# First score unit of each attention set in front of the last projected block of the stage before, in a decoder layer on one core

## The chip, the core and the metric

The kernel runs on one core of one Trainium2 chip. Five engines work side by side, each through its own queue in order: PE (TensorE: matrix products, with its weight loads shown apart as PEld), DVE (VectorE), ACT (ScalarE), POOL (GpSimd) and SP (SyncE, which here issues transfers). Products land in PSUM, from where DVE or ACT move them to SBUF. The metric is the device time of one execution in microseconds (us).

## What is computed

One decoder layer over four sequences (b = 0 to 3) of 512 rows and 512 columns in float32, with 16 heads of 32:

```
x = x + self_attention(layernorm(x))          # causal, projections q, k, v, o with biases
x = x + cross_attention(layernorm(x), ctx, ctx)   # causal mask of -10000; keys and values are ctx itself
x = x + ffn(layernorm(x))
ffn(x) = relu(x @ W_up.T) @ W_down.T + sum(softmax(top2(x @ W_gate.T))) * (x @ W_expert)
```

Softmax subtracts the largest score of each row, so every attention makes its scores twice: once by query to find the maxima, and once by key to take exponentials.

## The kernel before

The rows and the columns are cut into four blocks of 128 each. A projected block is four products of 128x128 by 128x512 (`project` or `project_t`); in the trace each such float32 product is two records.

**Order.** The order on PE, DVE, ACT and POOL is the order in which the program issues its instructions (`tc.manual_schedule`). For each sequence b the self attention and then the cross attention run through two functions. `with_maxima` makes the maxima of one attention in ten units and puts products of another stage between the units, so that the engines that work on the scores have time. `attend` then makes the exponentials and the values in ten further units.

**A unit.** In both functions a unit takes one or two pieces (g, i): g is a group of four heads, i a block of 128 rows or columns. Its scores go to two tiles of PSUM, each a `pair` of banks; four pairs exist in all (`ps`, bufs=4) and go round in the order in which the program gives them up. In `maxima` ACT copies each of the two tiles to SBUF (L304, tag `pt`, six buffers), POOL masks the diagonal (L312), and DVE reduces (L324), as `jobs` that are issued while the next unit's products are. After the last piece of a group, `split` writes its maxima as three bfloat16 parts (L345 to L350), `rows` turns them by PE (L361) and a copy puts them in SBUF (L367). In `scores` PE makes the scores (L405) and subtracts the maxima (L416), ACT takes the exponential of each tile (L439), and POOL clears the masked half (L447).

**What stands between.** `steps` is the list of blocks that `with_maxima` spreads over its units by `due`: for the first self attention two query and key blocks and all values (`query_key`, `value`); for the self attentions of b = 1 and 2 the `ffn` of the sequence before (`share`, `up`, `gate`, `down`); for that of b = 3 expert blocks and two `up` blocks; for the cross attentions the query and key blocks of the next sequence, in b = 1 with expert blocks of b = 0 behind them, and in b = 3 the rest of the `ffn` of b = 2. Two neighbouring blocks of `value`, `up`, `down` and `expert`, and query and key of one block of columns, share one pair and are moved to SBUF together: values and `down` by DVE's additions (L685, L843), experts by DVE (`weigh`, L867, which also issues the output transfer on SP), `up` by ACT (L790), queries and keys by ACT (L645, L648), and the last two `down` rows of b = 2 by ACT (`aside`, L861), whose addition POOL does later out of `put_off`.

**The entry of `attend`.** It starts when all blocks are done. Units 0, 1 and 2 are scored in a row; then the values of unit 0 (L482) follow, then unit 3, the maxima of the group or groups that `late` names (L361 again), the values of unit 1, unit 4 and so on. The pair of a group's values is held until that group is finished. DVE adds up exponentials over the blocks of a group (`add_up`, L552), and PE sums them over rows (L558).

Of the kernel before, what the change touches and what calls it, by code (L numbers as in the profile page):

```python
# [26 lines left out]
def decoder_layer(  # L27
# [21 lines left out]
    nc = tc.nc  # L49
# [579 lines left out]
            nc.gpsimd.tensor_tensor(e.x[:, t, :], e.x[:, t, :], bo_sb, ALU.add)  # L629

    def query_key(e):
        b, made = e.b, {}
        e.q_t = act.tile([P, NC, S], F32, tag="q_t", name=f"qT_{b}")
        e.k_t = act.tile([P, NC, S], F32, tag="k_t", name=f"kT_{b}")

        def query(f):
            made[f] = pair(f"pm_qk{b}_{f}")
            yield from project_t(made[f][:, 0, :], wq_sb, e.xn_t, f)

        def key(f):  # L640
            yield from project_t(made[f][:, 1, :], wk_sb, e.xn_t, f)
            out(f)

        def out(f):
            nc.scalar.activation(  # L645
                e.k_t[:, f, :], made[f][:, 1, :], AF.Identity, bias=bk_sb[:, f : f + 1]
            )
            nc.scalar.activation(  # L648
                e.q_t[:, f, :],
                made[f][:, 0, :],  # L650
                AF.Identity,
                bias=bqs_sb[:, f : f + 1],
                scale=SCALE,
            )

        def half(n):

            if n == 0:
                made[0] = pair(f"pm_qk{b}_0")
            rows = slice(n * S // 2, (n + 1) * S // 2)  # L660
            for c in range(NC):
                nc.tensor.matmul(
                    made[0][:, 0, rows],
                    lhsT=wq_sb[:, c, :P],
                    rhs=e.xn_t[:, c, rows],
                    start=(n == 0 and c == 0),
                    stop=(n == 1 and c == NC - 1),
                    skip_group_check=True,
                )

        steps = [(lambda f=f, w=w: w(f)) for f in range(NC) for w in (query, key)]
        if b == 0:
            steps[:1] = [lambda: half(0), lambda: half(1)]
        return steps

    def value(e):
        b, made = e.b, {}
        e.v = act.tile([P, NT, D], F32, tag="v", name=f"v_{b}")

        def one(t):  # L680
            if t % 2 == 0:
                made[0] = pair(f"pm_v{b}_{t}")
            yield from project(made[0][:, t % 2, :], e.xn_t, wv_sb, t)
            if t % 2 == 1:
                nc.vector.tensor_tensor(  # L685
                    e.v[:, t - 1 : t + 1, :],
                    made[0],
                    bv_sb.unsqueeze(1).to_broadcast([P, 2, D]),
                    ALU.add,
                )  # L690

        return [(lambda t=t: one(t)) for t in range(NT)]
# [85 lines left out]
    def ffn(e):  # L778
        b, f_t, made = e.b, e.f_t, {}

        def up(f):
            if f == 0:
                made["h"] = act.tile(
                    [P, NC, S], F32, tag="o_t" if b != B - 2 else "f_t", name=f"hT_{b}"
                )
            if f % 2 == 0:
                made["u"] = pair(f"pm_u{b}_{f}")
            yield from project_t(made["u"][:, f % 2, :], wup_sb, f_t, f)
            if f % 2 == 1:
                nc.scalar.activation(made["h"][:, f - 1 : f + 1, :], made["u"], AF.Relu)  # L790
# [41 lines left out]
            nc.vector.tensor_reduce(made["rw"], ew, axis=AX.X, op=ALU.add)  # L832

        def down(t):
            if t % 2 == 0:
                made["d"] = pair(f"pm_d{b}_{t}")
            yield from project(made["d"][:, t % 2, :], made["h"], wdown_sb, t)
            if t == NT - 1 and b == B - 2:
                for n in range(2):
                    aside(f"d{b}_{n}", t - 1 + n, made["d"][:, n, :])  # L840
            elif t % 2 == 1:
                both = e.x[:, t - 1 : t + 1, :]
                nc.vector.tensor_tensor(both, made["d"], both, ALU.add)  # L843

        def expert(t):
            if b == B - 1 and t == NT - 1:
                yield from expert_parts(t)
                return
            last = b == B - 1 and t == NT - 2
            if t % 2 == 0:  # L850
                made["e"] = pair(f"pm_e{b}_{t}")
            yield from project(made["e"][:, t % 2, :], f_t, wexp_sb, t)
            for n in (0,) if last else (0, 1) if t % 2 == 1 else ():
                u = t - t % 2 + n
                weigh(u, made["e"][:, n, :], slice(0, D), nc.sync)

        def aside(name, t, ps):


            some = work.tile([P, D], F32, tag="xn", name=f"some_{name}", bufs=4)  # L860
            nc.scalar.copy(some, ps)  # L861
            xt = e.x[:, t, :]
            put_off.append(lambda: nc.gpsimd.tensor_tensor(xt, xt, some, ALU.add))
# [41 lines left out]
    def with_maxima(steps, a, first=0, norms=()):  # L905


        norms = list(norms)
        run(steps[:first])
        fill = matmuls(steps[first:])  # L910
        total = sum(1 if step.__name__ in ("share", "gate") else NC for step in steps[first:])

        units = []
        for g in range(0, NC, 2):
            units += [[(g, 1), (g + 1, 1)]]
            units += [u for k in (g, g + 1) for u in ([(k, 2), (k, 0)], [(k, NT - 1)])]

        lead = 2 if first else 0
        for _ in range(lead):
            next(fill)  # L920
        done, due, jobs, late = lead, float(lead), [], {3: NC - 1}
        todo = []
        for n, pieces in enumerate(units):
            new = a.maxima(pieces)
            if todo:
                todo.pop()(nc.gpsimd)
            if norms and n % 2 == 0:
                new.append(norms.pop(0))
            due += (total - lead) / len(units)

            count = round(due) - done
            for k in range(count):
                next(fill, None)
                done += 1
                if k == min(1, count - 1) and n in (5, 7):
                    jobs = a.rows((n - 5) // 2) + jobs
                if k == min(1, count - 1) and a.cross and n in (6, 8):
                    todo.append(a.masked(*a.masked_sums((n - 6) // 2)))
                if n == len(units) - 1 and k == count - (2 if count > 4 else 1):
                    if total >= 2 * len(units):  # L940
                        if a.cross:
                            a.rows(2)[0](nc.scalar.copy)
                    else:
                        late = {3: 2, 5: NC - 1}
                run(jobs[:1])
                jobs = jobs[1:]
            run(jobs)
            jobs = new
        for _ in fill:
            pass  # L950
        run(jobs)
        return late

    def attend(a, late):


        units = []
        for g in range(0, NC, 2):
            units += [[(g, 0)], [(g, 3), (g, 1)], [(g, 2), (g + 1, 2)]]
            units += [[(g + 1, 0)], [(g + 1, 3), (g + 1, 1)]]  # L960
        waiting, held, todo = [], [], []

        def values():
            made = waiting.pop(0)
# [8 lines left out]
                if waiting[0][0][1] == 2 and waiting[0][1][0] == a.joined:  # L973
                    a.join(waiting[0][1], waiting[1][0])

        for n, pieces in enumerate(units):
            waiting.append(a.scores(pieces))
            if n in late:
                two = a.cross and late[n] == NC - 1
                together = not a.cross and len(late) == 1  # L980
                both = pair(f"mt_{a.name}_both") if two or together else None
                copies = a.rows(2, both, 1) if together else []
                copies += a.rows(late[n], both)

                more = [a.masked_sums(2, both)] if two else []
                for copy in copies:
                    copy(nc.scalar.copy)
                todo.extend(a.masked(*each) for each in more)
            if a.cross and n == 7:
                todo.append(a.masked(*a.masked_sums(3)))  # L990
            if n in (4 if a.joined is None else 6, 6, 9) and todo:
                todo.pop(0)()
            if n in (3, 4) and put_off:
                put_off.pop(0)()
            if len(waiting) > 2:
                values()
        while waiting:
            values()
# [1 line left out]
    with tc.manual_schedule(engines=BY_HAND):  # L1000
# [11 lines left out]
        for b in range(B):  # L1012
# [2 lines left out]
            norms, turns = [], []  # L1015
            if more:
                after, norms, turns = norm_in(b + 1)
            late = with_maxima(between_self, sa, skip, norms)
            if b == B - 1:
                e.x = load_x(b)  # L1020
            attend(sa, late)
            if b > 0:
                add_bias(e)
            made = out_projection(e, sa, context(e) + turns)
# [4 lines left out]
            norm_cross(e, made, 2)  # L1029
            ca = Attention(e.cq_t, e.ck_t, e.cv, True, f"c{b}")  # L1030
            ca.e, ca.out = e, e.beh_t
            late = with_maxima(steps[3:], ca)
            if b + 2 < B:
                after.x = load_x(b + 1)
            attend(ca, late)
            if more:
                cvs[b + 1] = load_cv(b + 1)
            filler = value(after) if more else ahead
# [73 lines left out]
```

## Time and profile before

Three runs took 803.87, 804.10 and 805.67 us, median 804.1. The profiled execution is one further execution; of it the span is known, 803.7 us from its first to its last instruction, and no time of its own beside that. TensorE's granted clock was 0.998 over it.

| stretch, us | what it is | length | PE busy | DVE busy | ACT busy | POOL busy |
|---|---|---|---|---|---|---|
| 27.5 to 66.7 | maxima, self, b = 0 | 39.2 | 39.20 | 28.94 | 21.63 | 14.43 |
| 66.7 to 77.3 | entry of its `attend` | 10.6 | 10.39 | 10.45 | 8.55 | 5.55 |
| 126.3 to 157.3 | maxima, cross, b = 0 | 31.0 | 31.00 | 24.85 | 24.03 | 13.08 |
| 157.3 to 168.1 | entry of its `attend` | 10.8 | 10.44 | 10.06 | 10.18 | 8.97 |
| 309.5 to 354.4 | maxima, cross, b = 1 | 44.9 | 44.90 | 26.36 | 25.24 | 14.76 |
| 676.3 to 706.3 | maxima, cross, b = 3 | 30.0 | 30.00 | 25.74 | 21.83 | 13.60 |

A line of the timeline gives the start, the duration, the engine, the line of the kernel, the operation, what it writes and reads, its shape, and the number of instructions merged; in square brackets stands the idle time of the engine before it and what ended it. The ends of PE's instructions are modelled, so the distance from start to start says more than the duration. In the names, `sm` are scores for maxima, `sc` scores for exponentials, `pv` values, `mt` turned maxima, `mb` maxima summed for the masked part of the cross attention, `pm` projected blocks; `_s` is self, `_c` cross.

### The profile page before, as it was taken

How to read it: one execution, taken by the hardware profiler on the slowest of the kernel's cores; microseconds unless marked ns; L12 is line 12 of the kernel's file. 1: busy time of each engine (PE TensorE's matmuls, PEld its weight loads, DVE VectorE, ACT ScalarE, POOL GpSimd, SP SyncE). 2: the span in 40 equal slices, each digit the busy share in tenths (PEclk: the TensorE clock that was granted, in tenths of full speed). 3: DMA queues.
4: the chain of work that ended last, by engine and by line, in shares of the span. 5: the costliest groups of instructions: out<-in, count | busy, mean ns of one | idle time of the engine just before them, and what ended most of it. 6: DMA issues, size and time to landing. Idle time of an engine off the chain costs nothing.

```text
span 803.7 us, 13927 instructions
## 1 busy us (share of the span) xinstructions
PE 794.0 (99%) x5588; PEld 378.9 (47%) x5592; DVE 565.9 (70%) x963; ACT 395.2 (49%) x448; POOL 339.6 (42%) x523
## 2 busy tenths in 40 slices
PE   8999999999999999999999999999999999999998
PEld 6444454444444454444544455444444444444544
DVE  2378855889679854678867786588959766988512
ACT  2457516871456615567055742687156833674110
POOL 3434612564234732257332482256423652475100
PEclk9999999999999999999999999999999999999999
DMA  9710000001010000021100000000102000000101
GB/s 301 275 28 1 2 1 1 2 27 54 1 27 2 2 0 1 2 78 55 53 14 14 1 2 0 1 1 2 53 28 80 2 1 1 1 2 1 53 1 52
DMA packets 15282, 24.51 MB, mean 30 GB/s; under 512 B 2033, under 2 KB 5361, under 8 KB 15217
## 3 DMA queue, kind: packets, MB, share of 16 engines
q1 hardware_dynamic: 14496, 22.96, 8.6%
q8 instruction: 44, 0.72, 0.4%
q10 hardware_dynamic: 720, 0.66, 0.2%
q14 instruction: 22, 0.17, 0.1%
HBM read 19.42 MB, written 4.19 MB: 29 GB/s over the span
## 4 chain that ended last, share of the span: by engine, by line
PE 95%; ACT 2%; issue 1%; DMA 1%; DVE 0%; ACTq 0%
PE pm_qk L241 14%; PE pm_d L229 7%; PE pm_u L241 7%; PE pm_v L229 7%; PE pm_o L725 7%; PE pm_e L229 7%; PE pv_c L482 6%; PE pv_s L482 6%; PE sm_c L293 6%; PE sm_s L293 6%; PE sc_s L405 5%; PE sc_c L405 5%; PE sc_s L416 1%; PE sc_c L416 1%; PE tp_a L255 1%
## 5 line engine op out<-in xcount | busy, mean ns | idle before, releaser
L324 DVE TENSOR_REDUCE nm_s<-s_s 128x2 f32<-128x1024 f32 (+3 forms) x128 | 96.9, 810 | 34.7 <-POOL s_s L312 34.7
L324 DVE TENSOR_REDUCE nm_c<-s_c 128x2 f32<-128x1024 f32 (+3 forms) x128 | 95.8, 810 | 31.0 <-POOL s_c L312 31.0
L304 ACT COPY s_s<-sm_s 128x1024 f32<-128x1024 f32 x80 | 77.1, 1015 | 70.7 <-PE sm_s L293 36.7
L304 ACT COPY s_c<-sm_c 128x1024 f32<-128x1024 f32 x80 | 77.1, 1016 | 35.9 <-PE sm_c L293 16.2
L312 POOL TENSOR_SCALAR_AFFINE_SELECT s_c<-s_c 128x512 f32<-128x512 f32 (+1 forms) x80 | 43.9, 550 | 100.4 <-ACT s_c L304 100.4
L312 POOL TENSOR_SCALAR_AFFINE_SELECT s_s<-s_s 128x512 f32<-128x512 f32 (+1 forms) x80 | 43.8, 551 | 94.4 <-ACT s_s L304 94.4
L552 DVE TENSOR_TENSOR sum_s<-sum_s,pt_s 128x256 f32<-128x256 f32 (+2 forms) x72 | 59.9, 897 | 15.4 <-PE pv_s L482 15.4
L439 ACT ACTIVATE pt_c<-sc_c 128x1024 f32<-128x1024 f32 x64 | 61.7, 1031 | 18.1 <-PE sc_c L416 10.1
L447 POOL TENSOR_SCALAR_AFFINE_SELECT pt_c<-pt_c 128x512 f32<-128x512 f32 (+1 forms) x64 | 52.9, 833 | 20.7 <-ACT pt_c L439 20.2
L229 PE MATMUL pm_d<-wdown_sb,hT 128*128 128x512 f32 x128 | 61.5, 611 | 0.0
L241 PE MATMUL pm_qk<-xnT,wk_sb 128*128 128x512 f32 x128 | 61.0, 606 | 0.0
L241 PE MATMUL pm_u<-fT,wup_sb 128*128 128x512 f32 x128 | 59.3, 605 | 0.0
L439 ACT ACTIVATE pt_s<-sc_s 128x1024 f32<-128x1024 f32 x56 | 53.9, 1030 | 10.5 <-POOL pt_s L447 5.5
L229 PE MATMUL pm_v<-wv_sb,xnT 128*128 128x512 f32 x128 | 58.8, 600 | 0.0
L725 PE MATMUL pm_o<-wo_sb,oT_s 128*128 128x512 f32 x128 | 57.8, 596 | 0.0
L405 PE MATMUL sc_c<-cqT,ckT 32*128 32x384 f32 (+3 forms) x512 | 56.4, 464 | 0.9 <-ACT sum_c L439 0.9
L241 PE MATMUL pm_qk<-xnT,wq_sb 128*128 128x512 f32 x120 | 56.7, 605 | 0.0
L229 PE MATMUL pm_e<-wexp_sb,fT 128*128 128x512 f32 x120 | 56.3, 604 | 0.0
L447 POOL TENSOR_SCALAR_AFFINE_SELECT pt_s<-pt_s 128x512 f32<-128x512 f32 (+1 forms) x56 | 48.0, 865 | 16.9 <-ACT pt_s L439 16.2
L405 PE MATMUL sc_s<-qT,kT 32*128 32x128 f32 (+3 forms) x512 | 54.1, 464 | 0.9 <-ACT sum_s L439 0.9
L293 PE MATMUL sm_c<-ckT,cqT 32*128 32x512 f32 (+3 forms) x512 | 47.5, 460 | 0.0
L293 PE MATMUL sm_s<-kT,qT 32*128 32x512 f32 (+3 forms) x512 | 47.0, 461 | 0.0
(171 smaller groups left out, 1268.1 us busy)
## 6 DMA issues: line engine op xcount, KB each, us to landing
cv<-in_ctx_dram SPq DMA_DIRECT2D x16, 256.0 KB, 4.4
out_dram<-x SPq DMA_DIRECT2D x15, 256.0 KB, 2.0
xin<-in_x_dram SPq DMA_DIRECT2D x12, 256.0 KB, 2.8
x<-in_x_dram SPq DMA_DIRECT2D x12, 256.0 KB, 4.2
wq_sb<-in_wq_dram SPq DMA_DIRECT2D x2, 512.0 KB, 6.7
wk_sb<-in_wk_dram SPq DMA_DIRECT2D x2, 512.0 KB, 7.7
wv_sb<-in_wv_dram SPq DMA_DIRECT2D x1, 1024.0 KB, 7.8
wo_sb<-in_wo_dram SPq DMA_DIRECT2D x1, 1024.0 KB, 9.5
```

Of the source, the lines that this page charges most:

```text
L229: nc.tensor.matmul(pm, lhsT=lhs_t[:, c, t * P : (t + 1) * P], rhs=w[:, c, :], start=(c == 0), stop=(c == NC - 1),)
L241: nc.tensor.matmul(pm, lhsT=w[:, c, f * P : (f + 1) * P], rhs=rhs_t[:, c, :], start=(c == 0), stop=(c == NC - 1),)
L293: nc.tensor.matmul(scs[r // 2][:, r % 2, c : c + (i + 1) * P], lhsT=self.q_t[h, g, i * P : (i + 1) * P], rhs=self.k_t[h, g, : (i + 1) * P] ...
L304: nc.scalar.copy(s, scs[n])
L312: nc.gpsimd.affine_select(out=diagonal, in_=diagonal, compare_op=ALU.is_ge, fill=NEG, base=0, pattern=[[0, 2], [0, len(pieces)], [-1, P]], ...
L324: nc.vector.tensor_reduce(self.nm[g][:, i, 2 * n : 2 * n + 2], made[n][:, :, c : c + (i + 1) * P], axis=AX.X, op=ALU.max, negate=True,)
L405: nc.tensor.matmul(scs[r // 2][:, r % 2, c : c + S - j * P], lhsT=self.k_t[h, g, j * P : (j + 1) * P], rhs=self.q_t[h, g, j * P :], start= ...
L439: nc.scalar.activation(pt, scs[n], AF.Exp)
L447: nc.gpsimd.affine_select(out=diagonal, in_=diagonal, compare_op=ALU.is_ge, fill=0.0, base=0, pattern=[[0, 2], [0, len(pieces)], [1, P]], ...
L482: nc.tensor.matmul(pv[r * HD : (r + 1) * HD, u, j * P :], lhsT=ones if u else self.v[:, j, h * HD : (h + 1) * HD], rhs=pts[r // 2][:, r % ...
L552: nc.vector.tensor_tensor(to, to, pts[n][:, :, c : c + S - j * P], ALU.add)
L725: nc.tensor.matmul(pms[t // 2][:, t % 2, :], lhsT=a.out[:, c, t * P : (t + 1) * P], rhs=wo_sb[:, c, :], start=(c == 0), stop=(c == NC - 1),)
```

## The change

Five edits, all in the order of work and in the use of PSUM pairs:

- `with_maxima` takes the last block out of the list that it spreads over the units: four products fewer stand between the units. After the units and the blocks that are left it issues score unit 0 of the attention, then the four products of the last block, with the reductions of the last maxima unit between them, and in an early cross attention the turned maxima of group 2. It returns unit 0 as `begun`.
- `attend` starts with `begun`, scores unit 1, and issues the values of unit 0 right behind it; unit 2 has no values behind it, and from unit 3 on the order is as before.
- The first stage issues six products instead of two before its first maxima unit.
- The last two blocks of a stage no longer share a pair, nor one instruction that moves them: the values 2 and 3 of b = 0, the first two `up` of b = 2, the last two `down` of b = 0 to 2, the experts 2 and 3 of b = 0, and query and key 3 of b = 1 and 3.
- Where the last query and key are apart, the query is moved right after its products.

```diff
     def query_key(e):
-        b, made = e.b, {}
+        b, made, apart = e.b, {}, (NC - 1,) if e.b % 2 else ()
...
         def query(f):
             made[f] = pair(f"pm_qk{b}_{f}")
             yield from project_t(made[f][:, 0, :], wq_sb, e.xn_t, f)
+            if f in apart:
+                out_query(f)
 
         def key(f):
-            yield from project_t(made[f][:, 1, :], wk_sb, e.xn_t, f)
-            out(f)
-
-        def out(f):
+            if f in apart:
+                pm = pair(f"pm_k{b}_{f}")[:, 0, :]
+            else:
+                pm = made[f][:, 1, :]
+            yield from project_t(pm, wk_sb, e.xn_t, f)
             nc.scalar.activation(
-                e.k_t[:, f, :], made[f][:, 1, :], AF.Identity, bias=bk_sb[:, f : f + 1]
-            )
+                e.k_t[:, f, :], pm, AF.Identity, bias=bk_sb[:, f : f + 1]
+            )
+            if f not in apart:
+                out_query(f)
...
+            if b == 0 and t >= NT - 2:
+                pm = pair(f"pm_v{b}_{t}")[:, 0, :]
+                yield from project(pm, e.xn_t, wv_sb, t)
+                nc.vector.tensor_tensor(e.v[:, t, :], pm, bv_sb, ALU.add)
+                return
...
+            if b == B - 2 and f < 2:
+                pm = pair(f"pm_u{b}_{f}")[:, 0, :]
+                yield from project_t(pm, wup_sb, f_t, f)
+                nc.scalar.activation(made["h"][:, f, :], pm, AF.Relu)
+                return
...
         def down(t):
+            if t >= NT - 2 and b < B - 1:
+                pm = pair(f"pm_d{b}_{t}")[:, 0, :]
+                yield from project(pm, made["h"], wdown_sb, t)
+                if b == B - 2:
+                    aside(f"d{b}_{t}", t, pm)
+                else:
+                    nc.vector.tensor_tensor(e.x[:, t, :], pm, e.x[:, t, :], ALU.add)
+                return
...
+            if b == 0 and t >= NT - 2:
+                pm = pair(f"pm_e{b}_{t}")[:, 0, :]
+                yield from project(pm, f_t, wexp_sb, t)
+                weigh(t, pm, slice(0, D), nc.sync)
                 return
...
     def with_maxima(steps, a, first=0, norms=()):
-        norms = list(norms)
-        run(steps[:first])
-        fill = matmuls(steps[first:])
-        total = sum(1 if step.__name__ in ("share", "gate") else NC for step in steps[first:])
...
-        lead = 2 if first else 0
+        norms = list(norms)
+        run(steps[:first])
+        fill, last = matmuls(steps[first:-1]), matmuls(steps[-1:])
+        total = sum(1 if step.__name__ in ("share", "gate") else NC for step in steps[first:-1])
+        early = total + NC >= 2 * len(units)
+
+        lead = 6 if first else 0
         for _ in range(lead):
             next(fill)
-        done, due, jobs, late = lead, float(lead), [], {3: NC - 1}
+        late = {3: NC - 1} if early else {3: 2, 5: NC - 1}
+        done, due, jobs = lead, float(lead), []
...
-                if n == len(units) - 1 and k == count - (2 if count > 4 else 1):
-                    if total >= 2 * len(units):
-                        if a.cross:
-                            a.rows(2)[0](nc.scalar.copy)
-                    else:
-                        late = {3: 2, 5: NC - 1}
...
         for _ in fill:
             pass
+        begun = [a.scores([(0, 0)])]
+        for k in range(NC):
+            next(last)
+            if k == 1 and a.cross and early:
+                a.rows(2)[0](nc.scalar.copy)
+            run(jobs[:1])
+            jobs = jobs[1:]
+        for _ in last:
+            pass
         run(jobs)
-        return late
+        return begun, late
...
-        waiting, held, todo = [], [], []
+        waiting, held, todo = list(begun), [], []
...
-        for n, pieces in enumerate(units):
+        for n, pieces in enumerate(units[1:], 1):
             waiting.append(a.scores(pieces))
...
-            if len(waiting) > 2:
+            if n == 1 or n > 2:
                 values()
```

## The prediction

> **What bounds the kernel now.** I read the page first: one engine is busy for the whole span.
>
> ```profile
> span 803.7 us, 13927 instructions
> PE 794.0 (99%) x5588; PEld 378.9 (47%) x5592; DVE 565.9 (70%) x963; ACT 395.2 (49%) x448; POOL 339.6 (42%) x523
> ```
>
> A busy PE is not a PE at its peak, and the view of waits gives PE almost none. So I read the start times in the timeline. The entry of the first self attention (PE, then ACT, then DVE):
>
> ```profile
> 66.70 1.14 PE L405 MATMUL sc_s<-qT,kT 32*128 32x512 f32 x8
> ...
> 69.16 0.70 PE L405 MATMUL sc_s<-qT,kT 32*128 32x256 f32 x4
> 70.07 0.92 PE L405 MATMUL sc_s<-qT,kT 32*128 32x256 f32 x10 [0.21 <-ACT sum_s L439]
> ...
> 71.35 1.07 PE L482 MATMUL pv_s<-sum_s,v 128*32 128x512 f32 x8
> 72.35 1.17 PE L405 MATMUL sc_s<-qT,kT 32*128 32x512 f32 x6
> ...
> 74.10 0.62 PE L361 MATMUL mt_s_both<-identb,parts 128*128 128x128 bf16 x8
> 74.65 1.07 PE L482 MATMUL pv_s<-pt_s,v 128*32 128x128 f32 x16
> 75.65 1.50 PE L405 MATMUL sc_s<-qT,kT 32*128 32x128 f32 x16
> ...
> 77.29 1.07 PE L482 MATMUL pv_s<-pt_s,v 128*32 128x256 f32 x16
> ```
>
> ```profile
> 68.08 1.94 ACT L439 ACTIVATE sum_s<-sc_s 128x1024 f32<-128x1024 f32 x2 [2.08 <-PE sc_s L416]
> 69.91 3.78 ACT L439 ACTIVATE pt_s<-sc_s 128x1024 f32<-128x1024 f32 x4
> 74.02 1.94 ACT L439 ACTIVATE sum_s<-sc_s 128x1024 f32<-128x1024 f32 x2 [0.33 <-PE sc_s L416]
> ```
>
> ```profile
> 66.81 1.23 DVE L685 TENSOR_TENSOR v<-pm_v,bv_sb 128x1024 f32<-128x1024 f32 x1
> ...
> 69.79 2.33 DVE L324 TENSOR_REDUCE nm_s<-s_s 128x2 f32<-128x1024 f32 x2
> 72.16 0.45 DVE L346 CAST parts<-nm_s 128x16 bf16<-128x16 f32 x1
> ```
>
> Score units 0 to 2 take 66.70 to 71.35, 4.65 us. An undisturbed unit takes 1.29 after values (79.28 to 80.56), 1.07 of it work; three in a row need 3.43. Units 3 and 4 take 1.75 and 1.64. So each entry, from unit 0 to the third values, takes 10.59 us, some 2.0 of it held by PSUM: four pairs of banks go round, and a unit needs two that ACT has emptied. All eight entries show 10.59, but c0 and c2 10.72, where ACT is late with keys and queries. In front of them, a unit of maxima with k products costs 1.07+0.20+0.86k: 2.98 for two (126.36 to 129.34), 3.84 for three. Where only one product stands between two units (the last cross attention), PSUM holds PE there too:
>
> ```profile
> 701.18 1.13 PE L229 MATMUL pm_d<-wdown_sb,hT 128*128 128x512 f32 x2
> 702.14 0.38 PE L374 MATMUL mb_c<-mrow_c,same 128*128 128x512 bf16 x1
> 702.45 1.98 PE L293 MATMUL sm_c<-ckT,cqT 32*128 32x512 f32 x8
> 704.36 1.98 PE L229 MATMUL pm_d<-wdown_sb,hT 128*128 128x512 f32 x4
> ```
>
> The last unit takes 1.91 instead of 1.07: its second half waits for ACT's copy of the unit before (to 703.26).
>
> I call the attentions s0, c0, s1 ... c3. The program hands PSUM pairs out in the order in which it gives them up. I follow that order by hand below, with the durations above. Median 804.1 is 0.4 above the profiled span; the change is inside the span, and I add its sum to 804.1.
>
> **The entry (eight times).** Unit 0 goes between projected products: 1.07+0.41 = 1.48, the second switch included. The last block (3.43) covers its exponentials. The trace has no score unit there; bounds are 1.07 (its share in a row of three) and 1.60 (a unit of 1.07 plus the 0.53 that a return shows at most); I take the maxima unit's value, which has the same shape. From unit 1 at 0: unit 1 to 1.46; its exponentials 1.48 to 3.42 (0.97 each); values of unit 0 to 2.46; unit 2 to 3.84; its exponentials 3.91 to 5.85. Unit 3 starts at 3.84, but the values hold one pair, so its second half needs unit 2's first: 4.92, and ends 1.27 later (as 72.83 to 74.10) at 6.19. Transposes 6.74, values 7.74. Unit 3's exponentials end at 7.08 and 8.04, so unit 4 ends at 8.09+1.33 = 9.42. With unit 0: 10.90 against 10.59, **+0.31** (c0 and c2: +0.18). The same recurrence gives the old entry its 4.65 and 10.59. The stall goes from unit 2 to units 3 and 4, because these now stand together. At no hold at all it would be 1.48+7.72 = 9.20, -1.39; the upper end is 11.02.
>
> The Trainium skill, "TensorEngine Tiling (Array Packing)", Key Properties, says that a change of tiling mode drains TensorE. That speaks against a unit set apart; by the row, the switches cost 0.41 x 8 = 3.3. The page has no price; were switches free, by it the sum would be 3.3 lower.
>
> **The last block's own pair.** Its emptying stands last in program order, and unit 2 needs that pair. On ACT (c0, c2, c3 and s3) it takes 0.6 to 0.7 before unit 1's exponentials: hidden, at zero; with ACT late it would cost that 0.7 each. On DVE (s0, s1, s2, c1) it queues behind the last reductions and the split (L346 to L350), while unit 2 waits.
> s0: DVE worked from 50.57 to the split at 72.16; less its one idle gap (0.81) and half of the old two-row addition (0.52), the new split starts at 70.83, takes 0.8 to 1.5, and the addition (0.68) ends at 72.3 to 73.0, say 72.7. Unit 2 would be ready at 66.70+1.48+2.46 = 70.6. From there to the third values 6.96: 79.65 against 77.29, **+2.35** in all (+0.31 to +2.7).
> s1, s2: the gate's reductions start at 230.7; 22.7 of DVE work (26.6 of before less 1.25 idle, 1.45 done earlier, 0.52 moved, 0.7 of slow casts) and 0.65 end at 254.05, against 253.88. **+0.5** each (-0.3 to +1.6); the two short stalls of 0.32 and 0.25 that the new spacing removes there only lengthen this wait.
>
> **Thinner spacing of the maxima (four fewer products in the ten units).** c0 and c2 have 16 instead of 20: per unit 2,1,2,1,2,2,1,2,1,2. ACT needs 1.93 per unit, plus 1.27 per query and key block and 0.69 per masked count. The rule, from 702.45 to 704.36: a copy starts 0.15 after its unit has ended, takes 0.97 a pair, and a half that waits for it lets the unit end 1.10 later. Followed from 126.36, holds are 0.1, 0.2, 0.1 in units 2 to 4; 0.84 in unit 7 (at 145.5, copy of unit 6 ends 146.31, the size of the row above); 1.2 in unit 8 (its pair is the second query and key block's, emptied at 150.7); 0.86 in unit 9. **+3.2** each, +3.4 with the entry. Bounds: 0 (units of two products show none) and 4 x 1.2 = 4.8.
> s3: two per unit instead of 2.4; the third projection up needs the pair of the last two expert rows, weighed on DVE (1.32; DVE was idle 3.6 before 599.0, and works on without a gap from there) by 613.65 while PE is there at 612.4: **+1.15** (0 to 1.3). c1: the same for the last maxima at 346.9 and a weighing to 347.35: **+0.45** (0 to 0.5). c3: 13 instead of 17; the third row down needs the pair of the first two, whose addition DVE, continuous from 680.42, reaches behind unit 4's reductions and split by 697.1, while PE is there at 695; some comes back, since the entry already ended on DVE's sums (L552 to 718.67): **+0.5** in all (-0.7 to +2). s0's 2.2 products a unit are like c0's two: zero (up to 0.84, the row above, where a copy of maxima by DVE, L367, keeps its pair longer); its lead of six instead of two delays DVE by 3.4, into an idle 3.3 before 50.23.
>
> **Rest.** Split rows: two of 0.6 for one of 1.02 to 1.23, DVE and ACT have room outside the places above. SP issues the same output DMAs, the third expert row earlier and the fourth some 1.5 us later; the load of x behind them is used over 100 us later. POOL gets unit 0's two selects (0.42) before the last block instead of after; nobody waits. The two deferred additions keep their place. The late transposes (L361) need the last split: 6.2 after unit 1, 3 us of slack in c0.
>
> **Sum.** s0 2.35; s1 and s2 1.0; c0 and c2 6.8; c1 0.75 (0.45+0.31); s3 1.45 (1.15+0.31); c3 0.5: +12.9. 804.1+12.9 = **817.0 us**.
>
> **Rivals.**
> 1. Faster: PSUM pairs come round in time. For it: PE is told to wait only 1.8 us in the wait view for all entries. Against: four instructions start at 69.16 and the next only at 70.07, when the exponential of unit 0 has ended. Price: entry -1.39 x 8 = -11.1, other terms zero: 793. It decides once unit 3 takes about 1.3 rather than 2.35 and units of one product 1.1.
> 2. The entry costs +0.31, the thin units are free and only DVE's gate holds: 8 x 0.31 + 2.05 + 0.4 = +4.9, 809. For it: behind two of c3's three one-product units the next unit lost only 0.15. Against: the 0.84 behind the third, the one that also had a masked count, as two of c0's four will.
> 3. No change: unit 0 costs only 1.07 and every added hold is zero, 8 x (10.49-10.59) = -0.8: 803. For it: the products around unit 0 leave DVE and ACT 3.4 us more before unit 1. Against: the return of 0.20 shows after every maxima unit.
> 4. DVE slower everywhere (casts at 0.66 instead of 0.20 when POOL works): s1 and s2 +1.6, s0 +2.7, c3 +2, and c0 and c2 4.8+0.2: with c1 and s3 as above 2.7+3.2+2+10+2.2 = +20, 824.
>
> **How the numbers follow.** Forecast 0.58 (811 to 822), rival 2 0.16, rival 1 0.10, rival 3 0.08 (0.05 of it within 0.2%, 0.02 below, 0.01 above), rival 4 0.08. Leaving out rival 1, the low half of 3 and most of 4 gives 804 to 823. About 0.2% (1.6 us) is what a measurement can tell from no change: faster 0.12, within 0.05, slower 0.83.
>
> **What would show it.** After the change: unit 1 of s0 at 68.2; unit 2 of s0 starting at 72 to 73 with DVE's addition to v just before; unit 3 of every entry with 2.3 us; maxima units 7 to 9 of c0 at 1.9, 2.3 and 1.9; c0's score unit 1 35.7 us after its first maxima unit (162.05 for 126.36). I'd be wrong if the pairs go round in another order, or if unit 0 costs 1.07 and units 3 and 4 show no hold.

## The result and the profile after

The changed kernel takes 814.81 us (median of four, 813.7 to 816.68) where the kernel before took 804.03 beside it (four, 803.87 to 805.67): a ratio of 1.013, 95% interval 1.0112 to 1.0148. It is 10.8 us slower; 817.0 was predicted, range 804 to 823. The page of the kernel after, with the chain that ended last:

```profile
span 812.0 us, 13931 instructions
PE 798.0 (98%) x5588; PEld 374.4 (46%) x5592; DVE 563.5 (69%) x966; ACT 397.1 (49%) x449; POOL 337.8 (42%) x523
...
PE 86%; DVE 10%; issue 2%; ACT 1%; DMA 0%; POOL 0%; ACTq 0%
```

PE's busy time went from 794.0 to 798.0 and the span by twice as much; so only a part of the loss shows as an idle PE, and the rest stands inside rows that last longer because a part of them waited (unit 7 below). DVE holds 10% of the chain; before, it held none of it.

The loss is best read by stage. The next table takes each attention with what follows it, from its first unit of maxima to that of the next attention (c3 to the end of the span), as a difference to the same stretch of the profile before. In s0 four products now stand ahead of the first unit instead of behind it, and their 3.44 us (4 x 0.86) are added back.

| | s0 | c0 | s1 | c1 | s2 | c2 | s3 | c3 | sum |
|---|---|---|---|---|---|---|---|---|---|
| predicted | +2.35 | +3.4 | +0.5 | +0.75 | +0.5 | +3.4 | +1.45 | +0.5 | +12.9 |
| after | +3.32 | +2.35 | -0.28 | +0.60 | -0.27 | +2.35 | +1.71 | +0.64 | +10.4 |

The spans differ by only 8.3, because the profiled execution of before came 2.08 us later to its first unit of maxima, the four products taken out. Apart from those products the change does nothing ahead of it. Most of the 2.08 is TensorE's clock, which read 0.57 over 4 us (an estimate: 4 x 0.43 = 1.7 us lost), as it did in the profile of experiment 8 (0.58), which starts with the same work as that of experiment 7 (1.00). (Columns: stretch and its length in us, PE's busy time and instructions, granted clock, share of the DMA engines, GB/s; first before, then after.)

```profile
8.00:12.00 4.00, 3.42 (x17) 0.57 1.14 343
```

```profile
8.00:12.00 4.00, 3.97 (x25) 1.00 1.07 356
```

With that taken out, the stages give 10.4. The medians give 10.8, but two of the four runs after took 813.70 (9.7 above the median before) and two 815.91 and 816.68, and no trace shows what set them apart.

**The entry.** PE in s1 of the kernel after, from unit 0 to the third values:

```profile
249.56 1.14 PE L405 MATMUL sc_s<-qT,kT 32*128 32x512 f32 x8
...
250.84 3.70 PE L229 MATMUL pm_d<-wdown_sb,hT 128*128 128x512 f32 x8
254.47 1.15 PE L405 MATMUL sc_s<-qT,kT 32*128 32x128 f32 x16
...
259.43 0.70 PE L405 MATMUL sc_s<-qT,kT 32*128 32x512 f32 x2 [0.30 <-ACT pt_s L439]
...
263.90 1.07 PE L482 MATMUL pv_s<-pt_s,v 128*32 128x256 f32 x16
```

From 249.56 to 254.47 are 4.91; less the block's four products (3.43) unit 0 costs 1.48. From unit 1 (254.47) to the third values (263.90) are 9.43. Together 10.91 against 10.59. The stall of unit 2 is gone (it takes 1.18 from 256.92), and unit 3 has it now: its second half starts at 259.43 and waits for ACT's exponentials, and the unit takes 2.61 to the turned maxima at 260.71, where it took 1.75 before. Unit 4 takes 1.64 as before.

**s0.** PE and DVE at the same place one sequence earlier (the two engines merged by time):

```profile
68.18 1.06 PE L482 MATMUL pv_s<-sum_s,v 128*32 128x512 f32 x8
...
70.31 0.69 DVE L350 TENSOR_TENSOR parts<-rest_s,parts 128x16 bf16<-128x16 f32 x1
70.87 0.68 DVE L691 TENSOR_TENSOR v<-pm_v,bv_sb 128x512 f32<-128x512 f32 x1
...
71.61 1.15 PE L405 MATMUL sc_s<-qT,kT 32*128 32x256 f32 x16 [2.36 <-DVE v L691]
```

Unit 2 needs the pair of the last projected block. DVE empties it last, behind the reductions and the split (L346 to L350), and PE stands idle for 2.36.

**c0.** Units 7, 8 and 9 of the maxima last 1.91, 1.44 and 1.74 instead of 1.07, each from its start to the start of PE's next row (148.60, 152.18 and 155.19):

```profile
146.69 1.98 PE L293 MATMUL sm_c<-ckT,cqT 32*128 32x512 f32 x8
...
150.74 1.51 PE L293 MATMUL sm_c<-ckT,cqT 32*128 32x384 f32 x16
...
153.45 1.81 PE L293 MATMUL sm_c<-ckT,cqT 32*128 32x512 f32 x8
```

Ahead of the second of these, ACT empties the pair of the second query and key block:

```profile
150.35 0.71 ACT L655 ACTIVATE qT<-pm_qk,bqs_sb 128x512 f32<-128x512 f32 x1
```

**s3.** The third `up` block waits for DVE's weighing of the last two expert rows:

```profile
618.38 1.40 DVE L894 SCALAR_TENSOR_TENSOR x<-pm_e,rw,x 128x512 f32<-128x512 f32 x2
```

```profile
619.84 1.98 PE L241 MATMUL pm_u<-fT,wup_sb 128*128 128x512 f32 x4 [1.39 <-DVE x L894]
```

### The profile page after: what moved, and what is told of

Same layout as the page of the kernel before. It is cut to its first block, busy times and chain, and to the rows that moved or that the text cites. A ratio compares the mean times of both kernels' runs of the same rounds, so it can differ in the third digit from the quotient of the medians.

```text
span 812.0 us, 13931 instructions
## 1 busy us (share of the span) xinstructions
PE 798.0 (98%) x5588; PEld 374.4 (46%) x5592; DVE 563.5 (69%) x966; ACT 397.1 (49%) x449; POOL 337.8 (42%) x523
## 4 chain that ended last, share of the span: by engine, by line
PE 86%; DVE 10%; issue 2%; ACT 1%; DMA 0%; POOL 0%; ACTq 0%
PE pm_qk L241 13%; PE pm_u L241 7%; PE pm_o L737 7%; PE pv_c L482 6%; PE sm_c L293 6%; PE pm_e L229 6%; DVE nm_s L324 6%; PE sc_c L405 6%; PE pv_s L482 5%; PE pm_v L229 5%; PE sc_s L405 4%; PE pm_d L229 4%; PE sm_s L293 3%; PE sc_c L416 1%; PE sc_s L416 1%
## 5 line engine op out<-in xcount | busy, mean ns | idle before, releaser
L552 DVE TENSOR_TENSOR sum_s<-sum_s,pt_s 128x256 f32<-128x256 f32 (+2 forms) x72 | 59.6, 887 | 28.7 <-PE pv_s L482 22.0
L447 POOL TENSOR_SCALAR_AFFINE_SELECT pt_s<-pt_s 128x512 f32<-128x512 f32 (+1 forms) x56 | 49.9, 901 | 34.9 <-ACT pt_s L439 34.2
L241 PE MATMUL pm_qk<-xnT,wk_sb 128*128 128x512 f32 x112 | 54.9, 611 | 0.0
L293 PE MATMUL sm_c<-ckT,cqT 32*128 32x384 f32 (+3 forms) x512 | 51.9, 460 | 0.0
L552 DVE TENSOR_TENSOR sum_c<-sum_c,pt_c 128x256 f32<-128x256 f32 (+2 forms) x48 | 42.7, 949 | 10.7 <-POOL pt_c L447 10.7
```

The lines of the kernel that those rows point to most:

```text
L241: nc.tensor.matmul(pm, lhsT=w[:, c, f * P : (f + 1) * P], rhs=rhs_t[:, c, :], start=(c == 0), stop=(c == NC - 1),)
L293: nc.tensor.matmul(scs[r // 2][:, r % 2, c : c + (i + 1) * P], lhsT=self.q_t[h, g, i * P : (i + 1) * P], rhs=self.k_t[h, g, : (i + 1) * P] ...
L447: nc.gpsimd.affine_select(out=diagonal, in_=diagonal, compare_op=ALU.is_ge, fill=0.0, base=0, pattern=[[0, 2], [0, len(pieces)], [1, P]], ...
L552: nc.vector.tensor_tensor(to, to, pts[n][:, :, c : c + S - j * P], ALU.add)
```

## The experiments

My theory was that the loss has three separate sources: PSUM pairs that DVE empties late (s0, s3), units of maxima that stand too close together once four products are taken from between them (c0, c2), and an entry that only moves its stall. The rivals were that moving unit 0 itself is what costs, and that the number of products alone decides, wherever they stand. The stages of every run, as differences to before in the same way (in the run with the longer lead six products are added back in s0):

| run | s0 | c0 | s1 | c1 | s2 | c2 | s3 | c3 | sum |
|---|---|---|---|---|---|---|---|---|---|
| after | +3.32 | +2.35 | -0.28 | +0.60 | -0.27 | +2.35 | +1.71 | +0.64 | +10.4 |
| 1 reductions behind the block | +0.96 | +2.36 | -0.34 | +0.60 | -0.34 | +2.35 | +1.72 | +0.64 | +7.9 |
| 2 thin spacing only | +0.96 | +2.09 | -0.60 | +0.35 | -0.60 | +2.09 | +1.46 | +0.93 | +6.7 |
| 3 values a unit later | +4.92 | +1.76 | -0.33 | +0.01 | -0.33 | +1.76 | +1.12 | +0.97 | +9.9 |
| 4 two units ahead | +1.67 | +1.15 | -0.77 | -0.60 | -0.77 | +1.15 | +0.51 | +0.82 | +3.1 |
| 5 other dealing | +4.36 | +1.36 | -0.27 | +0.60 | -0.28 | +1.35 | +1.72 | +0.65 | +9.5 |
| 6 longer lead | +0.93 | +2.35 | -0.34 | +0.60 | -0.34 | +2.35 | +1.71 | +0.65 | +7.9 |
| 7 two ahead in s1, c1, s2 | +0.01 | +0.01 | -0.78 | -0.60 | -0.78 | 0.00 | +0.01 | 0.00 | -2.1 |
| 8 in c0, c2, s3 too | +0.02 | +0.15 | -0.78 | -0.61 | -0.78 | +0.14 | +0.08 | +0.01 | -1.8 |
| 9 as 7, emptied first | 0.00 | +0.01 | -1.55 | -0.60 | -1.55 | 0.00 | 0.00 | 0.00 | -3.7 |

A stage that an edit leaves alone repeats within 0.1, except s0 in run 5 (see the end), so these differences of single profiles can be trusted to about that.

### 1. The last reductions behind the last block

```diff
         for k in range(NC):
             next(last)
...
-            run(jobs[:1])
-            jobs = jobs[1:]
         for _ in last:
             pass
         run(jobs)
```

> The change, with the reductions and the split of the last maxima unit issued behind the last block instead of between its products. Theory (in s0 unit 2 waits because the addition that empties the last block's pair stands on DVE behind the last reductions): the 2.4 us between the values of unit 0 and unit 2 in s0 go, everything else stays within 0.3 us a stage; -2.3 us in all. Rival (unit 2 waits there for ACT or for the exponentials, and the DVE name is chance): s0's entry stays at 11.7 us from unit 1 to the third values, 0 in all.

Measured: 812.15 in one run. s0 is 2.36 shorter than after, and the largest other difference is 0.07. DVE now adds the last values at 67.92, right behind unit 0's block, and unit 2 follows the values of unit 0 at once:

```profile
67.92 0.69 DVE L691 TENSOR_TENSOR v<-pm_v,bv_sb 128x512 f32<-128x512 f32 x1
```

```profile
70.11 1.31 PE L405 MATMUL sc_s<-qT,kT 32*128 32x256 f32 x16
```

So the 2.36 of s0 is the order on DVE, and nothing else in the kernel depended on it: in s1 and s2 the same order costs only 0.06.

### 2. Thin spacing only

The last block stands right behind the units of maxima, and scores 0 to 2 in a row behind it; its pair is still its own, and the maxima are still spread over four products fewer.

```diff
-        begun = [a.scores([(0, 0)])]
         for k in range(NC):
             next(last)
...
-            run(jobs[:1])
-            jobs = jobs[1:]
         for _ in last:
             pass
         run(jobs)
-        return begun, late
+        return [a.scores([(0, 0)])], late
...
-            if n == 1 or n > 2:
+            if len(waiting) > 2:
                 values()
```

> Only the thinner spacing: the last block stays out of the units and stands behind them, but score unit 0 follows it, units 0 to 2 are scored in a row and the values come as before; the last reductions are issued behind the block so that DVE's emptying holds nobody. Theory (the thin units alone cost what the maxima stages lost): c0 and c2 keep +2.2 each over before, s3 +1.5, s0 about +0.8, c1 +0.3, s1 and s2 -0.45 each, the entries are 10.6 to 10.8 us as before; about +6 us over before in all. Rival (the moved unit disturbs the stage): maxima holds vanish, within 1 us of before.

Measured: 811.44 (four runs), ratio 1.0083, interval 1.0063 to 1.0103; stages +6.7. That is nearly two thirds of the loss with unit 0 back in its old place. The step from this run to run 1 (6.7 to 7.9) is what setting unit 0 apart costs at the entry: some 0.26 in six stages, nothing in s0, and 0.3 less in c3. The rival that the moved unit is the cause falls. Three sources add up: spacing and own pairs 6.7, entry 1.2, DVE's order 2.5. How the 6.7 divides between thinner spacing and own pairs, no run separates.

### 3. The first values a unit later

Unit 0 stays ahead of the last block, but units 1, 2 and 3 are treated as before: values follow once three units wait.

```diff
-            if n == 1 or n > 2:
+            if len(waiting) > 2:
                 values()
```

> The change, with the values of unit 0 behind unit 2 again. Theory (the hold moved to units 3 and 4 because unit 2 and 3 stand together): from unit 1 to the third values 8.9 instead of 9.43 us, about -0.5 us in each of eight entries, -4 us in all; s0's wait for DVE stays. Rival (the cost of the entry is the extra switch of the array alone): no change, 0.

Measured: 813.34 in one run; by stages 0.5 less than after, where 4 was expected. c0, c1, c2 and s3 gain 0.59 each, as expected, s1 and s2 only 0.05, and c3 loses 0.33 later. s0 loses 1.6 more: unit 2 comes earlier than after, right behind unit 1, and so waits even longer for DVE (2.94 instead of 2.36). Part of that is a clock that fell behind the idle stretch: the values after unit 2 take 1.66 instead of 1.07 (last section). The miss was not to follow that the same pair is needed sooner.

### 4. Two units ahead of the last block

```diff
-        begun = [a.scores([(0, 0)])]
+        begun = [a.scores([(0, 0)]), a.scores([(0, 3), (0, 1)])]
...
-        for n, pieces in enumerate(units[1:], 1):
+        for n, pieces in enumerate(units[2:], 2):
...
-            if n == 1 or n > 2:
+            if len(waiting) > 2:
                 values()
```

> The change, with score units 0 and 1 both in front of the last block, values of unit 0 behind unit 2. Theory (an entry is held by the chain of exponentials through four PSUM pairs, and 3.4 us of products hide as many exponentials as are ready): the block covers four exponentials instead of two, units 2 and 3 find their pairs empty; entry without the block 9.2 us instead of 10.91, -1.7 us in each of eight, s0 about another -0.9: -14 us against the change, some 4 under before, the thin units' cost staying. Rival (exponentials need the same time wherever they stand, ACT is the bound of the entry): entry stays above 10.4, at most -4 us against the change.

Measured: 806.68 (ten runs), ratio 1.0031, interval 1.0021 to 1.0041; 7.3 less than after by stages, half of the expected 14. PE in c1:

```profile
352.51 1.14 PE L405 MATMUL sc_c<-cqT,ckT 32*128 32x512 f32 x8
...
365.87 0.42 PE L482 MATMUL pv_c<-pt_c,cv 128*32 128x256 f32 x4
```

From 352.51 to 365.87 are 13.36; less the block (3.43) and the transposes that moved into it (0.28: unit 0's end to unit 1 is 3.91 in c1 after, 3.63 in s1), 9.65 against 10.59. Two pairs of exponentials are hidden behind the block, and the long wait in unit 3 is gone; what is left is 0.2 in unit 3 and 0.35 in unit 4 (1.50 and 1.64 to 1.65 where 1.29 is undisturbed). That remainder is one reason for the miss. The other is that in s0, s1 and s2 the two units do not take 2.46 but 4.37, 3.24 and 3.23: the second needs a pair that DVE empties. In c3 they take 2.85, and there it is ACT's emptying of a `down` row (L888) that the second unit waits for. The thin stages keep their holds.

### 5. The same number of products, dealt out differently

```diff
             due += (total - lead) / (len(units))
+            if total == 16:
+                due = float((2, 3, 5, 6, 7, 8, 10, 12, 14, 16)[n])
```

> The change, with the 16 projected products between the ten maxima units of c0 and c2 dealt out as 2,1,2,1,1,1,2,2,2,2 in place of 2,1,2,1,2,2,1,2,1,2: the same number, but the two-product gaps lie where the masked counts and the second query and key block go. My theory: the holds in units 7 to 9 (0.84, 0.36 and 0.67 in c0) come from a one-product gap that also carries a masked count or the emptying of a query and key pair, so they go and some 0.2 to 0.8 may show in units 4 to 7 instead: c0 and c2 together 2 to 3 us shorter than with the change, the span about 809.5. Rival: four products fewer leave ACT short by a fixed amount, wherever they are missing: holds again 2.2 in each, the span as with the change (812). Nothing else differs; every other stage should be within 0.2 of the change's.

Measured: 813.02 in one run. c0 and c2 are 0.99 shorter each. Units 7 to 9 of c0 last 1.07, 1.16 and 1.07 (after: 1.91, 1.44, 1.74); in their place unit 6 lasts 1.81. Holds of 1.2 are left of 2.2: where the products stand matters, which the rival excluded, but half of the loss stays with this dealing too. Together the two stages gain 2.0, the low end of what was expected. s0 should have been as after and was 1.04 longer, again by the clock.

### 6. A longer lead in s0

```diff
-        lead = 6 if first else 0
+        lead = 8 if first else 0
```

made in the kernel of experiment 1. What it is about is a loss that the prediction does not contain. In s0 of the kernel after, unit 5 of the maxima takes 2.02 instead of 1.21, because it reads the last query and key block, which ACT empties just before:

```profile
45.33 0.70 ACT L655 ACTIVATE qT<-pm_qk,bqs_sb 128x512 f32<-128x512 f32 x1
```

```profile
46.09 0.71 PE L293 MATMUL sm_s<-kT,qT 32*128 32x256 f32 x8 [0.47 <-ACT qT L655]
```

> The kernel with the last reductions and the split behind the last block, and in s0 eight projected products ahead of the first maxima unit in place of six (20 instead of 22 between the units). My theory: in s0 maxima unit 5 lost 0.81 because it reads queries and keys of which the last ones are emptied just before, and with two products more ahead of it they are there: unit 5 back to 1.2, s0 0.8 shorter than in the run with the reductions behind the last block, so +0.15 over before instead of +0.96, all other stages within 0.1. Rival: unit 5 waits for ACT's copies of maxima, not for queries, and fewer products between the units make that worse: unit 5 stays at 2.0 or the loss goes to a later unit, s0 +0.9 to +1.8.

Measured: 811.41 in one run. Unit 5 is back to 1.08, so its cause was the query. But s0 is as long as in experiment 1 (+0.93, +0.96): the loss went to the gap behind unit 8, where the next value block waits for DVE.

```profile
56.00 1.21 DVE L697 TENSOR_TENSOR v<-pm_v,bv_sb 128x1024 f32<-128x1024 f32 x1
```

```profile
57.27 1.98 PE L229 MATMUL pm_v<-wv_sb,xnT 128*128 128x512 f32 x4 [0.90 <-DVE v L697]
```

My theory was right on the unit and wrong on the total; the rival's number came true with a third cause. The wait for DVE wasn't there in the kernel after. There the same block starts while the addition of the first two values (L697, from 56.17, lasting 1.22) is still running, so it can't have needed their pair:

```profile
57.06 1.98 PE L229 MATMUL pm_v<-wv_sb,xnT 128*128 128x512 f32 x4
```

Turned maxima take a pair too, and DVE's copy out of it (L367) stands ahead of that addition in the kernel after (55.84) and behind it here (57.13). So the longer lead changed the order in which the pairs come free, and the block got the pair that the addition empties. This reading fits both traces; no run tests it alone.

### 7. Two units ahead only where products are plenty

The kernel before, with the order of experiment 4 in s1, c1 and s2; the other stages run as before, so only the rows `down` of b = 0 and 1 and the experts of b = 0 get pairs of their own. The last reductions stand ahead of the last block's emptying and the split behind it (`k < 2`).

```diff
+    MOVED = ('s1', 'c1', 's2')
...
+        move = a.name in MOVED
...
+        if not move:
+            run(jobs)
+            return [], late
+        begun = [a.scores([(0, 0)]), a.scores([(0, 3), (0, 1)])]
+        for k in range(NC):
+            next(last)
...
+            if k < 2:
+                run(jobs[:1])
+                jobs = jobs[1:]
```

> The kernel before, with two score units ahead of the last block in s1, c1 and s2 alone (the stages that keep two or more products between maxima units without that block, and that had a gain in the run with two units ahead); s0, c0, c2, s3 and c3 are as before, pairs shared and spacing thick. My theory: the entry itself gains when two units stand ahead, and what made the run with two units ahead slower than before is only the holds of the thin stages; so s1 and s2 -0.8 to -1.5 each, c1 -0.6: 2.2 to 3.6 below before, 800.4 to 801.8. Rival: the gains in s1 and s2 in that run were work brought over from the slower stages around them, and alone they are nothing: 803.5 to 804.5.

Measured: 801.95 (five runs) against 804.27, ratio 0.9969, interval 0.9956 to 0.9981. The three stages keep exactly their gains of experiment 4, for s1 and s2 just short of the range (-0.78 against -0.8), and nothing changes elsewhere. So the move itself pays, and the gains were not brought over from slower neighbours.

### 8. The thin stages as well

Experiment 7 with c0, c2 (dealt as in experiment 5) and s3 moved too, and the last two expert rows of b = 1, which s3 carries, in pairs of their own (the text below calls b = 1 the third sequence; it is the second).

```diff
-    MOVED = ('s1', 'c1', 's2')
+    MOVED = ('s1', 'c1', 's2', 'c0', 'c2', 's3')
...
-            if (b == 0) and t >= NT - 2:
+            if (b < 2) and t >= NT - 2:
                 pm = pair(f"pm_e{b}_{t}")[:, 0, :]
```

> The kernel before that has two score units ahead in s1, c1 and s2, with c0, c2 and s3 moved as well: c0 and c2 with the other dealing of their 16 products, s3 with the last two expert rows of the third sequence in pairs of their own. My theory: c0 and c2 pay at most 0.8 of holds against 0.9 to 1.2 gained at the entry, so -0.4 each, and s3 without its 1.47 hold -1.0: 1.8 below the run with three stages moved, about 799. Rival: the thin stages cost as much as in the run with two units ahead (c0 and c2 +1.1 each, s3 +0.5): 2.7 above the run with three stages moved.

Measured: 803.24 (twelve runs), ratio 0.9983, interval 0.9973 to 0.9993. By stages 0.4 more than experiment 7, neither theory's number. The rest of the 1.3 between the medians isn't in the stages; these two profiles differ ahead of the first unit of maxima, which comes at 27.39 here and at 25.67 in experiment 7, with the same work in front of it. At c0 and c2 the gain at the entry and the holds cancel (+0.15). In s3 own pairs cut the 1.47 to two waits of 0.6 and 0.4, both for DVE's weighing (L897), which use up the entry's gain.

### 9. Emptied first

Experiment 7, with the reductions of s1's and s2's last gap behind the emptying of the second-last block's pair.

```diff
-                run(jobs[:1])
-                jobs = jobs[1:]
+                if not move or a.cross or n < len(units) - 1:
+                    run(jobs[:1])
+                    jobs = jobs[1:]
             run(jobs)
```

> The version with two score units ahead of the last block in s1, c1 and s2, where in s1 and s2 DVE's reductions of the last gap stand behind the emptying of the second-last block's pair. My theory: the 0.77 by which the two score units there last longer than in c1 (3.23 against 2.46) are the second unit's second half waiting for DVE's addition to x, which a reduction of 1.27 holds up: 2.46 in both, s1 and s2 0.7 shorter each, 1.4 in all, about 800.5. Rival: DVE has that much left to do whatever the order, and the wait goes to unit 2 or to the last block's own pair: s1 and s2 as before this edit, 802.

Measured: **800.03** (five runs) against 804.22, ratio 0.995, interval 0.9936 to 0.9963: 4.2 us faster than the kernel before. In s1, DVE and PE of experiment 7, where a reduction stands ahead of the addition:

```profile
244.13 1.27 DVE L324 TENSOR_REDUCE nm_s<-s_s 128x2 f32<-128x768 f32 x2
245.32 0.68 DVE L858 TENSOR_TENSOR x<-pm_d,x 128x512 f32<-128x512 f32 x1
```

```profile
246.06 1.14 PE L405 MATMUL sc_s<-qT,kT 32*128 32x128 f32 x12 [0.38 <-DVE x L858]
```

and of this run, where the addition is made at 244.26, ahead of the reductions (244.87), and PE does not wait:

```profile
244.26 0.69 DVE L858 TENSOR_TENSOR x<-pm_d,x 128x512 f32<-128x512 f32 x1
```

```profile
245.33 1.05 PE L405 MATMUL sc_s<-qT,kT 32*128 32x128 f32 x16
```

The two score units last 2.46 as in c1, and s1 and s2 are 0.77 shorter each. Unit 2 is not later for it.

## Where the prediction was right and where it failed

The direction and the case (the forecast, 811 to 822) were right, and so were the main mechanisms: the entry, DVE's gate in s0 and the holds of c0 and c2. The sum of 12.9 measured 10.4, and that hides errors of both signs, so a part of the nearness is luck.

- **Entry.** Right to 0.02 in s1 and s2: 1.48 for unit 0 and 9.43 from unit 1 (9.42 predicted); in c0, c1, c2, s3 and c3 it is 9.36 to 9.37. Inside, two misses cancel: unit 2 took 1.18 (1.38 predicted) and unit 3 2.61 (2.35). The stall went to unit 3 alone, not to units 3 and 4. Rival 1 (pairs come round in time) is out. The Trainium skill's "TensorEngine Tiling (Array Packing)", Key Properties, on the drain at a mode change, fits the 0.41 that unit 0 costs beyond its 1.07; no run here shows the drain by itself.
- **s0: DVE gate right, one wait missed.** Unit 1 was predicted at 68.2 and unit 2 at 72 to 73, "with DVE's addition to v just before". They came at 66.88 and 71.61, because this execution started 2.08 earlier and unit 5 took 0.81 back. From unit 1 to the third values are 11.71 (11.47 predicted), so this term is 2.6 and not 2.35: the split took 1.6 (69.25 to 70.87), where 0.8 to 1.5 was allowed. Experiment 1 removes 2.36 of it by the order on DVE alone. The step that failed is "s0's 2.2 products a unit are like c0's two: zero": unit 5 lost 0.81 to the query it reads. In experiment 6 that wait is gone and s0 loses as much to DVE, in another order of the pairs.
- **c0 and c2: mechanism right, two holds mis-sized.** Unit 7's 0.84 is exact. Unit 8 was taken at 1.2 and measured 0.37, unit 9 at 0.86 and measured 0.67, units 2 to 4 at 0.4 and measured 0.3: 2.2 instead of 3.2 (the items as written add up to 3.3). c0's score unit 1 came 34.70 behind the first unit (162.30, 127.60), 35.7 was predicted. Unit 8 began where it was expected, 23.14 behind the first unit (150.74, 127.60), but its pair was emptied at 151.06 (150.35+0.71), 23.46 behind it, where "emptied at 150.7" had put it 24.34 behind. ACT was 0.88 quicker than the chain of durations: its rows follow one another 0.1 sooner than they last (L648 starts at 149.76 and lasts 0.72, L655 starts at 150.35), which makes up a part of that. Experiment 5 supports that such holds come from where one-product gaps meet other work for ACT.
- **s1 and s2: wrong sign.** "+0.5 each" measured -0.28. The wait of unit 2 for DVE was there, and of the size in the sum (0.17, 254.05 less 253.88): in s1 unit 2 came 2.45 behind unit 1, where 2.30 does without a wait (experiment 1), right behind DVE's addition:

```profile
256.18 0.69 DVE L858 TENSOR_TENSOR x<-pm_d,x 128x512 f32<-128x512 f32 x1
```

```profile
256.92 1.16 PE L405 MATMUL sc_s<-qT,kT 32*128 32x256 f32 x16
```

What failed is "only lengthen this wait". The removed stalls (1.39 and 1.32 became 1.18 and 1.08) were a gain, because the addition was over at 256.87. That is 253.27 in the time of before (s1's first unit came at 210.35 instead of 206.75), 0.78 ahead of the 254.05 to which DVE's chain had been followed: too fine a margin for a sum of 23 us of work.
- **s3, c1, c3.** s3: the predicted place (the third projection up behind the weighing), 1.47 instead of 1.15. c1: 0.29 in unit 7, not 0.45 in unit 9; the unit (341.20 to 342.56) ends 1.13 behind ACT's emptying of a query and key pair (L655, to 341.43), so ACT fits as the cause and not the weighing on DVE. c3: +0.64 against +0.5, and that is luck. The predicted wait of the third row `down` did not come: the row starts at 703.55, while the addition of the first two (703.34, lasting 1.22) is running, so here the pairs did go round in another order than the one followed. In its place the entry costs 0.40, and behind the third values PE's sums (L558) end 0.47 later, behind DVE's last additions (L552); 0.29 came back in the maxima.
- **The base.** The prediction set its sum on a median said to lie 0.4 above the profiled span. Runs of before take some 2.0 more than their span, so the profiled execution was one of some 805.7, with the drop of the clock at its start shown above. Because the sum was made of differences, this did no harm.

Rival 2 (thin units free, only DVE's gate holds, 809) misses the holds, which are in the 6.7 of experiment 2. Rival 3 is out by unit 0's 1.48. Rival 4 predicted all of DVE's casts slow; the last split of s0 shows 0.55 and 0.69 where 0.2 is usual, and those of c3 up to 1.11, but s1 and s2 do not. Over the whole trace, 24 of the 128 rows of splits (L346 to L350) take over 0.3, and all 24 overlap work on POOL; before, it was 26, and all overlapped too. So slow rows came with POOL's work, as the rival said, but no more often.

## What to carry to other kernels

Filler that is taken from one place to cover another is paid for where it is taken: price the gaps that become thinner first, above all those that also carry work for the engine that empties PSUM. When work is set ahead of a block, the block's own buffer becomes part of the path, so on the engine that empties it this must be issued ahead of longer work that nobody waits for yet. And a move that loses as a whole may win in the stages that have work to spare: here the same idea, with two units instead of one and in three of eight stages, is 4.2 us faster.

## What the hardware showed beyond that

An idle stretch of TensorE can cost more than its length. In s0, PE idles 2.36 in front of unit 2. In the profile after, the granted clock stayed at 1.00. In experiment 5, with the same instructions and the same gap there, it fell to about half within the next 4 us:

```profile
70.00:72.00 2.00, 0.11 (x4) 1.00 0.00 0
72.00:74.00 2.00, 2.00 (x24) 0.51 0.03 8
74.00:76.00 2.00, 2.00 (x18) 0.63 0.02 4
```

That made s0 1.04 longer: from unit 2 to the turned maxima PE takes 4.83 there (71.89 to 76.72) and 3.79 after (71.61 to 75.40). In experiment 3 (idle 2.94) the clock read 0.86, 0.50 and 0.79 in the six us from 72 to 78. The Trainium skill, "TensorE: Matmul & The Clock Gate", Part 1, tells of a gate with two states that falls to half speed after an idle window of about 3.4 us, and of windows that run free of the kernel's start. The half speed and the chance in it agree with these runs; by matmuls the gap here was only 2.4 to 2.9 us (3.27 and 3.34 by weight loads), so for the length the measurement decides.
